# Moving the left operands of the weight products to other SBUF addresses in a two-layer graph kernel

## The chip, the cores and the metric

The kernel runs on one NeuronCore of one Trainium2 chip. The metric is the device time of one execution in microseconds. The kernel before takes 2596.89 us (median of three runs, 2596.37 to 2597.45). All timed runs told below were in the fast state; runs with a single time have no state of their own and are used for their traces only.

## The reference

For each of 128 graphs with 128 nodes and 512 features there are two layers. Cut to the products:

```
h  = relu(layernorm(x))
# layer 0: two hypergraph convolutions, H = (adj != 0)
xw = h @ W1.T                      # 512 -> 1024
h1 = relu(Dn * (H @ (Be * (H.T @ xw))) + b1);  h1 = layernorm(h1)
y  = Dn * (H @ (Be * (H.T @ (h1 @ W2.T)))) + b2   # 1024 -> 512
x  = x + (y + h)
# layer 1: mean aggregation
h  = relu(layernorm(x))
x  = x + relu(concat(h, (adj @ h) / deg) @ W.T)   # two 512 -> 512 products
```

## The kernel before

Each product with a weight is made of three passes in the type fp32r. In the trace of the kernel before, one fp32r matmul of 512 columns is one record and follows the last after 229 to 233 ns; py, a matmul of the same shape in full fp32, is two records of 428 ns each. An operand is split in a high part h, a low part l and a part d made of both, whose product brings in the cross terms, so each product is h with h, l with l, d with d. Per graph there are 24 such matmuls with w1 (left operand z), 24 with w2 (nh, nl, nd) and 24 with w3 (hh, hl, hd). Each multiplies a 128x128 left operand, which is loaded into the array (the records LDWEIGHTS, 128x128, in the trace), with 512 columns of weights, which stream through it (the records MATMUL, 128x512).

```
const = ctx.enter_context(tc.tile_pool(name="const", bufs=1))
pool = ctx.enter_context(tc.tile_pool(name="pool", bufs=1))
...
def parts(tag):
    return {m: const.tile([P, KH, 512], FP, name=tag + m) for m in "hld"}
w1, w2, w3 = parts("w1"), parts("w2"), parts("w3")
...
def product(left, w, k0, kk, main, name, between=None):
    wr = [w[m].bitcast(FR) for m in "hld"]
    pm, pd = bank(name + "m"), bank(name + "d")
    for i in range(2):
        for k in range(kk):
            nc.tensor.matmul(pm, left[i](k), wr[i][:, k0 + k, :], ...)
    main(pm)
    if between:
        between()
    for k in range(kk):
        nc.tensor.matmul(pd, left[2](k), wr[2][:, k0 + k, :], ...)
    return pd
```

In the names of the profile, rm and rd are the results with w1, gm and gd those with w2, bm, bd, am and ad those with w3. ps_s, pz, py and the second pair named ad (line 490) are full fp32 matmuls between them. A step of the loop works on several graphs at different stages and holds 86 matmul instructions.

## Time and profile before

| | kernel before |
|---|---|
| time | 2596.89 us |
| span of the profiled run | 2596.6 us |
| TensorE busy | 97% |
| VectorE, ScalarE, GpSimd busy | 80%, 72%, 53% |
| granted clock, mean | 0.989; 1.00 in the steady part |
| one step | 19.52 us |
| TensorE in the chain that ended last | 95% |

"Pitch" in what follows is the time from the start of one matmul to the start of the next. The lines, and how they are read, are in the prediction below.

### The profile page before, as it was taken

What the parts mean: (1) busy time and instruction counts of PE and PEld (TensorE: products, weight loads), DVE (VectorE), ACT (ScalarE), POOL (GpSimd) and SP (SyncE); (2) the same over time, 40 slices, a digit from 0 to 9 for tenths busy, and PEclk for the clock granted to TensorE, in tenths of its full rate; (3) what the DMA queues carried; (4) which work ended last, traced back from release to release, by engine and by line L of the source; (5) the groups of instructions that cost most, each with busy time, mean ns of one, the idle gap of its engine ahead of it and who ended that gap; (6) DMA issues with size and microseconds to landing.
All of it is one profiled execution on the core that took longest, in us unless ns stands there. A gap on an engine that the chain in (4) does not pass through costs nothing.

```text
span 2596.6 us, 38459 instructions
## 1 busy us (share of the span) xinstructions
PE 2529.4 (97%) x11024; PEld 1986.1 (76%) x11024; DVE 2076.6 (80%) x4519; ACT 1867.0 (72%) x3872; POOL 1368.7 (53%) x921
## 2 busy tenths in 40 slices
PE   4799999999999999999999999999999999999997
PEld 3577777777777777777777777777777777777775
DVE  7788888887888887887888888888887888888874
ACT  4677767777767777777777777777777777777773
POOL 5555455455455455455455455555555555555552
PEclk8899999999999999999999999999999999999998
DMA  4443443343443343443443343343343343344331
GB/s 117 115 124 115 127 124 115 127 125 115 126 124 116 125 126 112 126 128 113 126 125 115 125 126 117 121 125 121 118 129 119 118 128 121 115 128 123 115 123 64
DMA packets 410292, 311.71 MB, mean 120 GB/s; under 512 B 177376, under 2 KB 341216, under 8 KB 410080
## 3 DMA queue, kind: packets, MB, share of 16 engines
q1 hardware_dynamic: 409248, 309.19, 38.4%
q8 instruction: 87, 1.43, 0.2%
q14 instruction: 125, 1.02, 0.1%
q10 hardware_dynamic: 576, 0.07, 0.0%
q0 software_dynamic: 256, 0.01, 0.0%
HBM read 166.47 MB, written 142.61 MB: 119 GB/s over the span
## 4 chain that ended last, share of the span: by engine, by line
PE 95%; DVE 2%; DMA 1%; ACT 1%; SPq 1%; issue 0%; POOL 0%; DVEq 0%; POOLq 0%; ACTq 0%
PE gm L328 18%; PE rm L328 18%; PE bm L328 9%; PE am L328 9%; PE gd L334 9%; PE rd L334 9%; PE bd L334 5%; PE ad L334 5%; PE py L441 4%; PE pz L297 4%; PE ad L490 4%; PE ps_s L271 1%; DVE w2l L115 0%; DMA b_bc<-in_b_dram 0%; SPq L132 0%
## 5 line engine op out<-in xcount | busy, mean ns | idle before, releaser
L403 POOL TENSOR_TENSOR hl<-ht,hh 128x512 fp32r<-128x512 f32 x128 | 166.3, 1299 | 1058.8 <-DMA adjb<-in_adj_dram 659.7
L215 ACT ACTIVATE h<-x_t 128x512 f32<-128x512 f32 x256 | 162.0, 633 | 360.4 <-DVE x_t L444 310.4
L353 POOL TENSOR_TENSOR r<-r,b_bc 128x512 f32<-128x512 f32 x256 | 385.5, 1506 | 9.2 <-DVE r L352 7.0
L403 POOL TENSOR_TENSOR nl<-nt,nh 128x1024 fp32r<-128x1024 f32 x128 | 308.6, 2411 | 102.0 <-ACT nh L399 101.1
L347 ACT ACTIVATE r<-rm,dinv 128x512 f32<-128x512 f32 x256 | 175.1, 684 | 246.3 <-PE rm L328 246.2
L334 PE MATMUL gd<-w2d,nd 128*128 128x512 f32 x1024 | 310.4, 445 | 4.1 <-DVE nd L408 4.1
L328 PE MATMUL rm<-w1h,z 128*128 128x512 f32 x1024 | 290.5, 406 | 1.4 <-ACT z L304 1.4
L328 PE MATMUL rm<-w1l,z 128*128 128x512 f32 x1024 | 278.7, 394 | 1.7 <-ACT w1l L113 1.7
L334 PE MATMUL rd<-w1d,z 128*128 128x512 f32 x1024 | 277.5, 393 | 1.8 <-POOL w1d L118 1.8
L328 PE MATMUL gm<-w2h,nh 128*128 128x512 f32 x1024 | 262.0, 398 | 7.4 <-ACT nh L399 7.4
L334 PEld LDWEIGHTS gd<-w2d,nd 128*128 128x128 f32 x1024 | 193.1, 189 | 99.4 <-issue 30.9
L328 PE MATMUL gm<-w2l,nl 128*128 128x512 f32 x1024 | 260.0, 396 | 0.0
L328 PEld LDWEIGHTS gm<-w2h,nh 128*128 128x128 f32 x1024 | 193.7, 189 | 54.7 <-ACT nh L399 7.8
L310 DVE SCALAR_TENSOR_TENSOR z<-z 128x512 fp32r<-128x512 f32 x128 | 226.4, 1769 | 4.4
L328 PEld LDWEIGHTS gm<-w2l,nl 128*128 128x128 f32 x1024 | 192.5, 188 | 46.9 <-POOL nl L403 0.4
L334 PEld LDWEIGHTS rd<-w1d,z 128*128 128x128 f32 x1024 | 193.2, 189 | 45.4 <-POOL w1d L118 3.0
L328 PEld LDWEIGHTS rm<-w1l,z 128*128 128x128 f32 x1024 | 193.2, 189 | 45.3 <-ACT w1l L113 2.5
L226 ACT ACTIVATE h<-x_t,rs 128x512 f32<-128x512 f32 x256 | 208.3, 814 | 26.0 <-DVE rs L222 24.8
L328 PEld LDWEIGHTS rm<-w1h,z 128*128 128x128 f32 x1024 | 184.6, 190 | 34.8 <-ACT z L304 1.7
L352 DVE SCALAR_TENSOR_TENSOR r<-rd,dinv,r 128x512 f32<-128x512 f32 x256 | 190.4, 744 | 11.3 <-ACT r L347 2.2
L408 DVE SCALAR_TENSOR_TENSOR hd<-hh,hl 128x512 fp32r<-128x512 f32 x128 | 193.8, 1514 | 4.5 <-POOL hl L403 4.5
L307 DVE TENSOR_TENSOR z<-pz,z 128x512 fp32r<-128x512 f32 x128 | 88.5, 692 | 135.1 <-ACT z L304 135.1
(96 smaller groups left out, 5718.5 us busy)
## 6 DMA issues: line engine op xcount, KB each, us to landing
n_scratch<-r SPq DMA_DIRECT2D x128, 512.0 KB, 2.6
nb<-n_scratch SPq DMA_DIRECT2D x512, 128.0 KB, 2.8
x_t<-in_x_dram SPq DMA_DIRECT2D x128, 256.0 KB, 3.3
h_scratch<-h SPq DMA_DIRECT2D x128, 256.0 KB, 2.0
hb<-h_scratch SPq DMA_DIRECT2D x512, 64.0 KB, 2.0
out_dram<-x_t SPq DMA_DIRECT2D x128, 256.0 KB, 2.0
adj_t<-in_adj_dram SPq DMA_DIRECT2D x128, 64.0 KB, 1.9
an_scratch<-adj_t SPq DMA_DIRECT2D x128, 64.0 KB, 1.7
```

The lines of the kernel that those rows point to most:

```text
L215: copy(junk, src, func, accum_out=sm)
L226: copy(dst, src, func, bias=rs[:, 1:2], scale=rs[:, 0:1])
L297: nc.tensor.matmul(z[:, k * P : (k + 1) * P], H0[g][:, k * P : (k + 1) * P], S[g], start=True, stop=True)
L310: nc.vector.scalar_tensor_tensor(d, h, 2.0**-12, l, MUL, SUB)
L328: nc.tensor.matmul(pm, left[i](k), wr[i][:, k0 + k, :], start=(i == 0 and k == 0), stop=(i == 1 and k == kk - 1))
L334: nc.tensor.matmul(pd, left[2](k), wr[2][:, k0 + k, :], start=(k == 0), stop=(k == kk - 1), skip_group_check=True)
L347: lambda pm: copy(r, pm, AF.Copy, scale=dn[:, 1:2]), "r")
L352: nc.vector.scalar_tensor_tensor(r, PR.pop((g, half)), dn[:, 0:1], r, MUL, ADD)
L353: nc.gpsimd.tensor_tensor(r, r, b1_bc[:, cols], ADD)
L403: nc.gpsimd.tensor_tensor(SPLIT[key], a, h, SUB)
L408: nc.vector.scalar_tensor_tensor(t, h, 2.0**-12, low, MUL, SUB)
L441: nc.tensor.matmul(py, S.pop(g), G.pop(g), start=True, stop=True)
```

## The change

The change gives all left operands a pool of their own right behind the weights. The intent is that all start 32 bytes above a multiple of 64, as z alone did before. No instruction is added or removed.

```diff
     const = ctx.enter_context(tc.tile_pool(name="const", bufs=1))
+    left = ctx.enter_context(tc.tile_pool(name="left", bufs=1))
     pool = ctx.enter_context(tc.tile_pool(name="pool", bufs=1))
...
-            self.raw = pool.tile([P, n, 512], FP, tag=tag, name="raw")
+            self.raw = (pool if tag in "rA" else left).tile([P, n, 512], FP, tag=tag, name="raw")
...
-        Z[g] = z = pool.tile([P, 3, KD, P], FP, tag="z", name="z")
+        Z[g] = z = left.tile([P, 3, KD, P], FP, tag="z", name="z")
...
-        t = pool.tile([P, Q, width // P, B], FP, tag=tag, name=name + "b")
+        t = (left if tag == "t2" else pool).tile([P, Q, width // P, B], FP, tag=tag, name=name + "b")
...
-        nt = pool.tile([P, t.shape[2], P], FP, tag=tag, name=name + "t")
+        nt = left.tile([P, t.shape[2], P], FP, tag=tag, name=name + "t")
...
-            return pool.tile(shape, dtype, tag=tag, name=name).bitcast(FR)
+            return left.tile(shape, dtype, tag=tag, name=name).bitcast(FR)
...
-    eps_root = const.tile([P, 1], FP, name="eps_root")
+    eps_root = pool.tile([P, 1], FP, name="eps_root")
```

## The prediction

> **What bounds the kernel now.** I read the page first, then the table of stretches, then the chain of waits through one step, then TensorE's own timeline. The page and the table of stretches say whether anything but TensorE matters:
>
> ```profile
> PE 2529.4 (97%) x11024; PEld 1986.1 (76%) x11024; DVE 2076.6 (80%) x4519; ACT 1867.0 (72%) x3872; POOL 1368.7 (53%) x921
> ...
> PE 95%; DVE 2%; DMA 1%; ACT 1%; SPq 1%; issue 0%; POOL 0%; DVEq 0%; POOLq 0%; ACTq 0%
> ...
> 600.00:1100.00 500.00, 500.00 (x2206) 394.60 (x2205) 407.23 (x894) 369.10 (x769) 269.21 (x181) 1.00 0.39 121
> ```
>
> In the steady part TensorE is busy for all of the 500 us at a granted clock of 1.00, and the chain that ends last is TensorE for 95% of the span. VectorE, the next, is busy 407 of 500 us. So the time of the kernel is the sum of the pitches (start to start) of its matmuls, plus a head and a tail of some 135 us. The chain counts each piece without overlap, so one step (one of the 128 graphs in flight) can be read from it directly. Columns: start, us, engine and line, instructions.
>
> ```profile
> 1005.46 0.22 PE ps_s L271 x2
> 1005.68 1.85 PE rm L328 x8
> 1007.53 0.91 PE rd L334 x4
> 1008.44 1.83 PE rm L328 x8
> 1010.28 0.91 PE rd L334 x4
> 1011.19 0.86 PE py L441 x2
> 1012.05 0.89 PE pz L297 x8
> 1012.94 1.85 PE bm L328 x8
> 1014.79 0.93 PE bd L334 x4
> 1015.73 1.87 PE am L328 x8
> 1017.59 0.93 PE ad L334 x4
> 1018.53 3.73 PE gm L328 x16
> 1022.26 0.86 PE ad L490 x2
> 1023.12 1.86 PE gd L334 x8
> 1024.98 0.22 PE ps_s L271 x2
> ```
>
> From ps_s to the next ps_s is 1024.98 - 1005.46 = 19.52 us without a gap. The reader is to see one thing: the same instruction (128x128 left operand, 128x512 weights, one pass) does not have one price. The second rm with rd of the w1 product takes 1.83 + 0.91 = 2.74 us for 12, or 228.5 ns each. am with ad takes 1.87 + 0.93 = 2.80 us for 12, or 233.3 ns, and gm 3.73 us for 16, or 233.1 ns. The mean durations in the costliest groups (445 ns for gd, 406 for rm) do not show this: records of consecutive matmuls overlap, so a pitch has to be taken from starts.
>
> **Why the two prices differ.** In the built program all nine weight tiles start at 24,800 + n x 16,384 bytes in a partition, which is 32 above a multiple of 64. The left operand z starts at 216,992, also 32 above one. The other six start at multiples of 64: nd 189,696, nl 193,792, nh 197,888, hd 201,984, hh 204,032, hl 206,080. So in the kernel before, place and price go together: 32 above costs 229 ns, on the multiple 233.4. The single starts of the trace repeat it in the medians over 123 full steps: z's pitches cycle through about 229, 232 and 226 ns, the others' through 232 and 235. The head speaks for it too. There z runs with no other product before it, and at full clock it falls into its own cycle; w2 with nh does likewise into the other. It is confounded, though: z is also the only left operand of w1, and no trace of this kernel has w1 with another operand.
>
> At low clock both cost the same. Timeline of the head, while the clock is still down:
>
> ```profile
> 17.27 1.91 PE L328 MATMUL rm<-w1l,z 128*128 128x512 f32 x4
> ...
> 18.98 1.05 PE L334 MATMUL rd<-w1d,z 128*128 128x512 f32 x2
> ...
> 88.68 3.78 PE L328 MATMUL gm<-w2h,nh 128*128 128x512 f32 x8 [7.38 <-ACT nh L399]
> ...
> 92.26 2.23 PE L328 MATMUL gm<-w2l,nl 128*128 128x512 f32 x8
> ```
>
> z: (18.98 - 17.27) / 4 = 427 ns. nh: 92.26 - 88.68 = 3.58 us for eight, of which the first took 0.59 by its own starts, leaving 427 ns for each of seven. A penalty that shows only when columns stream at full rate looks like a collision of two reads of SBUF, the streaming weights and the left operand being loaded for the next matmul. That mechanism is my inference; the 4 ns are measured.
>
> **What the Trainium skill says.** "TensorE: Matmul & The Clock Gate", section "Back-to-back issue gap", gives N/2.4 + 2.5 ns for an isolated warm matmul, 216 ns at N = 512 (and about 131 per matmul in a sustained stream, which nothing here comes near). This trace shows 229 and 233, so 13 to 18 ns over the first figure, and at the low clock exactly its N/1.2 = 427. "SBUF — State Buffer", section "Who interferes with whom", gives TensorE two independent read ports, one for the moving operand and one for the load, and says that it never waits on anyone. The trace does not contradict that of other engines[...]. The same page, section "Operand start alignment", asks only for a multiple of the element size and says of its runs that they "timed nothing". So no page prices 32 against 64 bytes; the trace alone does.
>
> **The change, part by part.**
> 1. Instructions, order and waits: nothing changes. I compared the two built programs by engine, waits included, with line numbers and buffer numbers left out: no difference. Tags, and so the reuse of buffers, are the same; only pools, hence addresses, differ.
> 2. Addresses after: nd 172,256, nl 176,352, nh 180,448, hd 184,544, hh 186,592, hl 188,640, z 190,688. All seven are 32 above a multiple of 64. r, g, x_t and h0 move, but stay at multiples of 64; weights, s and ant keep their residue.
> 3. Matmuls that gain: 24 with w3 and 24 with w2 per graph, 48 x 128 = 6144 of the 11,024. If each paid z's steady price, the gain would be 233.4 - 229.1 = 4.3 ns x 6144 = 26 us.
> 4. What of it is lost at the start of a product: after a full fp32 matmul (pz, ps_s, L490) the pitch takes some matmuls to settle, and by the single starts z settles from above (233, 236, 229, 232) and hh from below (227, 235, 231, 229). So I compare like with like, by sums of the median starts. From the last fp32 pass, the 24 of w3 take 5.59 us, where z's 24 take 5.51: 0.08 saved. The 16 of gm take 3.736 us against 16 x 229.1 = 3.666: 0.07. The eight of gd take 1.861 us against z's first eight 1.852: 0.01. Sum 0.16 us per step of 19.52.
> 5. On the path: all of it, since TensorE has no idle in a step. 0.16 x 128 = 20.5 us, less a little for the head and the tail, where some 40 matmuls run at the low clock and gain nothing. 2597 - 20.5 = 2576.5; I take 2576.
> 6. Other work: the other engines get a step of 19.36 us and need at most 407/500 x 19.52 = 15.9 us of it (VectorE). Transfers that land in the moved raw tiles and nb now start 32 above a multiple of 64. hb already does, and lands in 2.0 us (64 KB) where nb takes 2.8 (128 KB), so I expect no cost; nb is not on the chain anyway.
>
> **Rivals.**
> A. The price belongs to w1, or to something else about z, not to the 32 bytes: the time stays at 2597. For it: the confounding named above. Against it: all nine weight tiles have the same residue and shape, and w2 and w3 agree with each other to 0.3 ns.
> B. What counts is the distance between left operand and weights, or a coarser multiple. Before, z was at 32 modulo 128 and the weights at 96; after, all are at 96, and their distance is a multiple of 2048 bytes. If the two reads then meet on the same place, pitches could rise for z as well: 72 x 4 ns x 128 = 37 us more, about 2634. Nothing in the trace shows such a case; small chance.
> C. The same, in the good direction: equal residues remove more of the 13 ns that z still pays over 216. If half of it went from all 72, 6.5 x 72 x 128 = 60 us would go beside the 20, to about 2517. Small chance too.
> D. Another engine becomes the bound, or the clock is throttled. VectorE has 18% of room and the clock is at 1.00 through the steady part, so no.
>
> **Range and chances.** About seven in ten for the mechanism, giving 2568 to 2582 according to how the products settle; two in ten for A near 2597; the rest for B and C. Eight times in ten the time should lie in 2566 to 2598. A change over 2% needs 52 us, which only C or a strong B could give: faster by over 2% 0.03, within 2% 0.94, slower by over 2% 0.03.
>
> **What would show it.** In the chain of the changed kernel, gm should take 3.66 to 3.68 us for 16 and am with ad 2.74 to 2.76 for 12, rm and rd unchanged, and a step 19.36 us; the durations on the other engines should stay. If gm stays at 3.73, rival A is right. If rm with rd moves from 2.74, the residue modulo 64 is not the whole rule.

## The result and the profile after

The changed kernel takes 2569.12 us (median of four runs, 2568.87 to 2570.42), the kernel before 2597.17 in the same rounds. The ratio is 0.9893, 95% interval 0.9876 to 0.9911. Ratios here are the mean time of one kernel's fast runs over that of the other's fast runs of the same rounds, so they are not quite the ratio of the medians quoted. A second measurement (run after_again) gave 2569.38 us and 0.9892. The gain is 28 us, 1.1%, inside the range and somewhat more than the 21 us forecast.

The chain of waits of the changed kernel, one step (start, us, engine and line, instructions; line numbers are one higher than before):

```profile
1013.95 0.22 PE ps_s L272 x2
1014.17 1.85 PE rm L329 x8
1016.02 0.91 PE rd L335 x4
1016.93 1.81 PE rm L329 x8
1018.74 0.91 PE rd L335 x4
...
1021.40 1.85 PE bm L329 x8
1023.24 0.92 PE bd L335 x4
1024.16 1.81 PE am L329 x8
1025.98 0.91 PE ad L335 x4
1026.88 3.62 PE gm L329 x16
...
1031.37 1.85 PE gd L335 x8
1033.21 0.22 PE ps_s L272 x2
```

The step is now 1033.21 - 1013.95 = 19.26 us. The reader is to see two things. First, am with ad takes 1.81 + 0.91 = 2.72 us for 12, 226.7 ns each, where 229 was expected. Second, the later rm with rd also takes 2.72 us, where it took 2.74. The w1 product has become cheaper too, although z was 32 above a multiple of 64 in both kernels. By single starts, the settled pitch is a constant 226.7 ns in all three products; the cycles of two and three values of the kernel before are gone.

The price of a product's start has not gone. After a full fp32 pass the pitches of the changed kernel run 229, 233, 236, 224, 231, 236, 228 and so on before they rest at 227. So the first eight of w1 and of w3 and all eight of gd still take 1.85 us.

The page's line on the chain and its row for the same 500 us as before:

```profile
PE 73%; ACT 9%; DVE 8%; DMA 4%; issue 3%; SPq 2%; POOL 1%; DVEq 0%; ACTq 0%; POOLq 0%
...
600.00:1100.00 500.00, 499.65 (x2231) 398.70 (x2230) 410.29 (x908) 372.80 (x778) 269.93 (x182) 1.00 0.41 124
```

TensorE was the chain for 95% of the span and is for 73% in this trace. That share is no property of the kernel: the same kernel, profiled again as after_again, has

```profile
PE 93%; DVE 2%; ACT 2%; DMA 1%; SPq 1%; issue 1%; POOL 0%; DVEq 0%; POOLq 0%; ACTq 0%
```

though it took 2568.57 us, as against 2569.05 us. A short wait can send the chain over the other engines for many steps back. What both traces show is that TensorE has begun to wait, though little: 499.65 of 500 us are busy here. One row of TensorE's waits, of the kernel before and then of the changed one (us in total, times, longest), and the chain at one such wait of the changed kernel:

```profile
PE py L441 <- POOL g L437: 7.7, 3, 3.6
```

```profile
PE py L442 <- POOL g L438: 10.5, 7, 3.9
```

```profile
933.49 3.33 DMA hb<-h_scratch
...
936.94 0.71 DVE ht L380
...
938.65 0.61 ACT hh L400
...
940.95 0.94 POOL g L438
...
941.94 1.12 PE py L442 x2
```

A transfer hb that usually lands in 2.0 us took 3.33; what depends on it came late and TensorE waited. Such slow landings are not new (the slowest hb took 3.9 us before and 4.0 after); what is new is that a step has less room for them. Added over the 122 steps between the first few and the end, the time above the median step is 0.20 us in the kernel before, 3.65 us in the changed one and 2.75 us in after_again. So the account for the two profiled executions is: 122 steps of 0.26 us less would be 31.7 us; 3.45 us of it were lost to new waits; head and tail became 1.4 us shorter. That makes 29.7 us, and the spans differ by 2596.6 - 2567.0 = 29.6 us. The timed medians differ by 28, because the profiled execution of the kernel before, 2598.55 us, was 1.4 us slower than the median.

### The profile page after: what moved, and what is told of

Its sections match the earlier page's. It is cut to its first block, busy times and chain, and to the rows that moved or that the text cites. A ratio compares the mean times of both kernels' runs of the same rounds, so it can differ in the third digit from the quotient of the medians.

```text
span 2567.0 us, 38459 instructions
## 1 busy us (share of the span) xinstructions
PE 2496.4 (97%) x11024; PEld 1982.6 (77%) x11024; DVE 2064.1 (80%) x4519; ACT 1866.1 (73%) x3872; POOL 1366.7 (53%) x921
## 4 chain that ended last, share of the span: by engine, by line
PE 73%; ACT 9%; DVE 8%; DMA 4%; issue 3%; SPq 2%; POOL 1%; DVEq 0%; ACTq 0%; POOLq 0%
PE gm L329 14%; PE rm L329 13%; PE bm L329 7%; PE am L329 7%; PE gd L335 7%; PE rd L335 7%; PE py L442 4%; PE bd L335 4%; PE ad L335 3%; PE pz L298 3%; PE ad L491 3%; DMA hb<-h_scratch 1%; DMA nb<-n_scratch 1%; ACT r L216 1%; ACT h L210 1%
## 5 line engine op out<-in xcount | busy, mean ns | idle before, releaser
L329 PE MATMUL gm<-w2h,nh 128*128 128x512 f32 x1024 | 255.6, 392 | 7.4 <-ACT nh L400 7.4
L329 PE MATMUL gm<-w2l,nl 128*128 128x512 f32 x1024 | 253.5, 390 | 0.0
```

The source lines that it names most:

```text
L329: nc.tensor.matmul(pm, left[i](k), wr[i][:, k0 + k, :], start=(i == 0 and k == 0), stop=(i == 1 and k == kk - 1))
```

## The experiments

Twelve kernels ran. The first four ask which property of the addresses counts. In e1 to e4, s1, s2 and f1 the built program has the same instructions, order and waits as the changed kernel (s1, s2 and f1 apart from how tiles are named and sliced). "Distance" below is the start of a left operand minus the start of its weights, modulo 256 unless another modulus is named. The pools were split into three (for nd to nh, for hd to hl, for z), with pads in front, and the weights could be moved by a pad before them:

```diff
-    left = ctx.enter_context(tc.tile_pool(name="left", bufs=1))
+    left = {c: ctx.enter_context(tc.tile_pool(name="left" + c, bufs=1)) for c in "thz"}
+    for c, pad in (("t", ...), ("h", ...), ("z", ...)):
+        if pad:
+            left[c].tile([P, pad // 4], FP, name="pad" + c)
...
+    pool.tile([P, 8], FP, name="padp")     # e1, e2, s1: keeps the tiles of pool on multiples of 64
...
+    const.tile([P, 8], FP, name="padw")     # only where the weights move by 32
```

**e1_swap: exchange the places of z and the others.** Pads of 192, 0 and 352 bytes: nd to hl at distance 192, z at 32.

> The left operands change places as seen from the weights: z (for w1) now starts 32 bytes past the residue of the weights modulo 512 and on a multiple of 64, as nd to hl did before; nd to hl start 192 past it, 32 above a multiple of 64, as z did before. Address theories (absolute residue or distance, both): the two prices change places, w1 products near 233.4 ns per matmul (12 in about 2.80 us), w2 and w3 products near 229.1 (16 of gm in 3.67 us), step about 19.42 us and time about 2584 us. Rival A of the prediction (w1 or z itself has the price): w1 stays at 229 or falls to 227 as in the changed kernel, w2 and w3 stay at 233.4, time near 2597 us.

Measured: 2586.83 us (one run), step 19.44 us. The chain:

```profile
1004.82 1.87 PE rm L333 x8
1006.69 0.93 PE rd L339 x4
...
1012.14 1.83 PE am L333 x8
1013.97 0.91 PE ad L339 x4
1014.88 3.66 PE gm L333 x16
```

The w1 product now pays 2.80 us for 12 (233.3 ns) and w3 2.74 (228.3); gm has come down to 3.66. The prices went with the addresses, so rival A of the prediction, that w1 or z itself had the price, is out.

**e2_all64: everything 32 bytes further.** Only the pad before the weights; the left pool follows. All operands are then on multiples of 64, and the distance stays 0.

> Weights and left operands all 32 bytes further than in the changed kernel: every one of them now starts on a multiple of 64 (left operands on a multiple of 128), and the distance of left operand to weights stays a multiple of 2048 bytes. Distance theory: 226.7 ns in every product, time as the changed kernel, 2569 us within 3. Absolute theory (left operands must lie 32 above a multiple of 64): 233.4 ns in all 72 products of a step, step near 19.62 us, time near 2610 us.

Measured: 2566.27 us (2565.39 to 2570.40), ratio 0.9882 (0.9868 to 0.9897). The chain has

```profile
1003.88 1.81 PE am L334 x8
1005.69 0.91 PE ad L340 x4
1006.60 3.63 PE gm L334 x16
```

which is 226.7 ns again for the 12 of w3. Lying 32 bytes above a multiple of 64 is not needed. The start of a product is another matter: after L496 (the changed kernel's L491) gd's pitches are 233 and 231 and then 227, where in the changed kernel all eight of gd stay unsettled, at the same distance of 0. So how long a product settles does not depend on the distance alone.

**e3_weights32: only the weights 32 bytes further.** The left operands keep their residue modulo 512, so the distance is 480 modulo 512, which is 224.

> Only the weights move by 32 bytes, to a multiple of 64; the left operands keep the residue of the changed kernel modulo 512 (32 above a multiple of 64, 96 modulo 128), so the distance becomes 480 modulo 512. Absolute theory: 226.7 ns as in the changed kernel, 2569 us. Distance theory: not 226.7; something like the 233.4 that the distance 32 had before, step 19.5 to 19.6 us, time 2595 to 2612 us.

Measured: 2609.90 us (2608.45 to 2611.08), ratio 1.0047 (1.0031 to 1.0064), step 19.62 us. The chain has

```profile
1012.47 1.87 PE rm L333 x8
1014.33 0.94 PE rd L339 x4
...
1022.62 3.74 PE gm L333 x16
```

2.81 us for 12 of w1 is 234 ns, 3.74 for 16 of w2 is 233.8 ns (233.3 by single starts, without the matmul at a product's end): all three products are slow now, although every left operand has the residue that the change aimed at. e2_all64 and e3_weights32 together decide for the distance and against the absolute place of the left operand.

**e4_far: three distances.** Pads of 64, 64 and 128 bytes: 64 for nd to nh, 128 for hd to hl, 256 for z.

> Weights as in the changed kernel; nd, nl, nh at a distance of 64 modulo 512 from them, hd, hh, hl at 128, z at 256. All stay 32 above a multiple of 64. If only the residue modulo 64 counts: all at 226.7 ns. If a modulus of 128 counts (z before had 64 modulo 128 and 229.1 ns): gm and gd at 229.1, w3 and w1 products at 226.7. If a modulus of 256: w1 alone at 226.7, w3 something else. If 512: none at 226.7. Time 2569 to 2600 us accordingly.

Measured: 2595.53 us (one run). w1 at 256 rests at 226.7 ns as at 0. w2 at 64 alternates between 231 and 236; w3 at 128 goes through a long cycle between 228 and 241, near 233 on average. All three are 32 above a multiple of 64, so the residue modulo 64 alone does not decide. Neither does a modulus of 128: 128 is not as good as 0. One of 256 fits.

**s1_fine and s2_fine: the remaining places.** The same pads with other values, and z sliced out of a slightly larger tile, so that it can start at any multiple of four bytes.

> Known so far, steady pitch by distance of left operand to weights modulo 256: 0 gives 226.7 ns, 32, 64 and 224 give 233.3 to 233.5, 128 about 233, 192 gives 229.2. Here nd to nh (w2) stand at 96, hd to hl (w3) at 160, z (w1) at 16. Theory: only the distance modulo 256 counts and 0 is the one good place: 96 and 160 lie between 229 and 234. At 16 the theory of whole 32-byte places says 226.7 (same place as 0), that of a finer grain says 229 to 234. If any of the three is under 226, a better place than that of the changed kernel exists.

> nd to nh (w2) stand at a distance of 128, hd to hl (w3) at 224, z (w1) at 240, modulo 256. Distance theory modulo 256, whatever the weight matrix: w2 at 128 as w3 had it (about 233 on average), w3 at 224 as all had it at 480 (233.3). A theory of modulo 512 would let w3 at 224 differ from 480. z at 240, 16 bytes short of the weights' place: 226.7 if 16 bytes do not matter on that side, 229 to 234 if they do.

Measured: 2594.46 and 2594.06 us (one run each, two of three products at bad places on purpose). In s1_fine, w2 at 96 took 233.8 ns, w3 at 160 233.4. z at 16 took 226.7 and, unlike at 0, from its second matmul on: its first twelve pitches are 313 and then 227 eleven times, where the changed kernel's are 318, 231, 236, 228, 233, 231 and only then 227. In s2_fine, w2 at 128 goes through the long cycle that w3 had there, w3 at 224 settles into the pitches of e3_weights32 to the ns (modulo 256, not 512), and z at 240 took 228.2. No place was under 226.7. The settled pitches, from the median starts over the 123 full steps of each trace (means over a cycle; where a cycle is cut moves them by up to 0.4 ns):

| distance modulo 256 | settled pitch, ns | product and run |
|---|---|---|
| 0 | 226.7 | all in the changed kernel and e2_all64; w1 in e4_far |
| 16 | 226.7, at once | w1 in s1_fine |
| 32 | 233.4 to 233.6 | w2, w3 before; w1 in e1_swap |
| 64 | 233.5 | w2 in e4_far |
| 96 | 233.8 | w2 in s1_fine |
| 128 | 232 to 233 | w3 in e4_far, w2 in s2_fine |
| 160 | 233.4 | w3 in s1_fine |
| 192 | 229.0 to 229.3 | w1 before; w2, w3 in e1_swap |
| 224 | 233.3 | all in e3_weights32; w3 in s2_fine |
| 240 | 228.2 | w1 in s2_fine |

Weights start on a multiple of 32 in all rows of the table.

**f1_all16: the distance 16 for all, by moving the weights.** It was meant as a kernel that beats both. A left operand is easily sliced at 16, but a shared tag is not, so I moved the weights: all nine in one tile that starts 16 bytes in.

```diff
+    pool.tile([P, 8], FP, name="padp")
+    flat = const.tile([P, 9 * KH * 512 + 8], FP, name="wall")[:, 4 : 4 + 9 * KH * 512]
+    every = flat.rearrange("p (w k c) -> p w k c", w=9, k=KH)
...
-        return {m: const.tile([P, KH, 512], FP, name=tag + m) for m in "hld"}
+        return {m: every[:, 3 * (int(tag[1]) - 1) + i] for i, m in enumerate("hld")}
```

> The changed kernel with every left operand 16 bytes past the place of the weights modulo 256 (all nine weight tiles in one tile that starts 16 bytes in; same instructions, order and waits). In the sweep z at 16 took 226.7 ns from its second matmul on, where at 0 it takes about ten to settle. If that holds for all: w1 saves 29 ns, w3 38 and gd 29 in a step, 96 ns together, step 19.16 us, time 2557 us. Rival: the step is by now so near to what the chain over DVE, ACT and the transfers needs that waits of py eat it: 2562 to 2569 us, not different from the changed kernel.

Measured: 2636.03 us (2635.09 to 2636.56), ratio 1.0149 (1.0132 to 1.0165), step 19.83 us. In the chain:

```profile
1013.31 3.79 PE gm L333 x16
```

That is 236.9 ns, by single starts an alternation of 234 and 239, 236.7 on average, in every product, with no wait added (instructions, order and waits are those of the changed kernel but for the names). Both theories of the expectation fell. At the same distance of 16, z in s1_fine took 226.7; the difference is that here the weights start 16 above a multiple of 32, and there z did. So the distance is not the whole rule: where the weights themselves start counts as well.

**after_again: the changed kernel in the same rounds.**

> The changed kernel itself, on the same chip and in the same rounds as f1_all16: 2569 us within 2, ratio to the kernel before 0.989.

Measured: 2569.38 us (2568.09 to 2571.01), ratio 0.9892 (0.9877 to 0.9906), as expected.

**f3_fine: 8 and 24 bytes.** f1_all16 with the tile cut at 24 bytes instead of 16, and z sliced 16 further.

> A finer grain: nd to hl at 8 bytes past the weights' place modulo 256, z at 24. If a grain of 32 bytes counts, all take 226.7 ns; if one of 16 bytes, w2 and w3 at 226.7 as at 0 with its settling, and z at 24 as at 16. Otherwise values between 226.7 and 233.4; a value under 226 would be a better place.

Measured: 2625.67 us (one run). w3 at 8 took 236.5 ns, w2 at 8 about 236, w1 at 24 233.3. Since the weights are off the multiple of 32 here too, the run does not answer what it was sent for. It agrees with f1_all16: in every product measured with weights off a multiple of 32 the pitch is between 233 and 237. Whether all weights off it are slow, with any left operand, is not shown.

**f4_next: which weights a left operand is measured against.** To tell a collision with the previous matmul's streaming from something about the pair itself, w1's high part and z's high part got steps of 2080 and 544 bytes from k to k in place of 2048 and 512.

```diff
+    odd = const.tile([P, 4 * 520 + 24 + 4 * 520], FP, name="w1h")   # two halves, step 520 elements
...
+        if w is w1:
+            left, wr = left[:1] * 3, [odd[k0 // KD].bitcast(FR)] * 3   # high parts thrice: wrong result
+            order, k0 = order[:: -1 if k0 else 1], 0
```

> Wrong results on purpose (w1 product with the high parts thrice), to tell which weights a left operand is measured against: its own, or those that stream while it is being loaded, which are the previous matmul's. In the first half of w1 each left operand stands at 0 from its own weights and at 32 (once in four at 160) from the previous ones; in the second half, with k reversed, at 32 from its own and at 0 (once in four at 128) from the previous ones. Theory that the load of the next left operand meets the streaming of the current weights: first half towards 233.4 ns, second half towards 226.7, with a longer pitch at most around every fourth. Theory of the own pair: the reverse, first half settling to 226.7, second half to 233.4. w2 and w3 are untouched controls at 226.7.

Measured: 2573.46 us (one run; the outputs still passed the comparison, presumably because the tripled product is normalised behind). In the chain the w1 product reads

```profile
1018.56 0.93 PE rd L345 x4
1019.49 1.84 PE rm L339 x8
1021.34 0.93 PE rd L345 x4
```

The second half, 2.77 us for 12, is 231 ns; the first half's settled matmuls, rd, take 231 too by single starts (0.93 us for four in the chain). w2 and w3 stay at 226.7. Neither half rests at 226.7 or at 233.4, so neither theory holds in its pure form. What it does show: an own distance of 0 in every matmul, as in the first half, does not suffice when the starts shift from one matmul to the next.

**e5_late_aggregate: one break fewer.** The full fp32 matmul of line 491 goes behind gd, so that gd follows gm directly.

```diff
-            conv2_weights(s - 1, between)
-        else:
-            between()
+            conv2_weights(s - 1, None)
+        between()
```

> The changed kernel with the full fp32 matmul of L491 (ad<-gb_t,ant) after the eight gd instead of between gm and gd, so that a step has two places instead of three where a product follows a full fp32 pass. Theory (the pitch has to settle after each such pass): gd takes 8 x 226.7 = 1.81 us instead of 1.85, w1 still settles; step 19.26 - 0.03 = 19.23 us, time 2565 us, 4 under the changed kernel. Rival (the settling belongs to the start of any product): no gain, 2569 us; or the later finish costs a wait and it gets slower than that.

Measured: 2725.78 us (2724.82 to 2726.66), ratio 1.0493 (1.0475 to 1.0510). From TensorE's waits:

```profile
PE py L442 <- POOL g L438: 122.2, 126, 5.5
```

The wait for g now comes in every step, 122 us in all, four times what the addresses gave. In the program VectorE's addition o (line 496), which needs the aggregate, stands ahead of its addition g (line 435), so a later aggregate makes g late. The trace shows, in one step, o waiting 1.13 us for the aggregate and starting at 1010.27 us, and g only at 1012.87. The median step is 1.26 us longer than in the changed kernel: by the single starts 1.05 us at the wait before py, 0.11 within py and 0.10 for the aggregate and gd. The expected gain is not there either: gd's first pitch is 332 ns, a gap of about 105, and the following ones are 231, 231, 233, 229, 231, 230 and 227. So the theory fell: gd pays a settling without a full fp32 pass before it; a short gap goes before it instead.

**e6_bias_first: take py's input out of the queue behind hl.**

```diff
-        do(layer1_low, s - 3)
         do(conv2_bias, s - 2)
+        do(layer1_low, s - 3)
```

> The changed kernel with the addition that py needs (conv2_bias, L438) before the subtraction hl (layer1_low, L404) on GpSimd. Theory: with the shorter step the changed kernel loses 3.65 us in some nine steps whose py waits for g, which stands behind hl, which waits for hh and so for the landing of hb; in front of hl it does not wait. Then those steps go, time 2565 to 2566 us. Rival: the lost time comes from a transfer that the whole step needs, the wait moves to bm on hl: 2569 us or a little over.

Measured: 2616.61 us (2612.45 to 2617.13), ratio 1.0070 (1.0055 to 1.0085), step 19.62 us. The waits of py did become fewer (5.0 us in two places), but hl, then hd, and all that stands behind hd on VectorE come later. TensorE is only 4% of the chain that ended last, VectorE 33% and ScalarE 30%. Between 1000 and 1060 us the chain is led by hd (9%) and goes by r, ScalarE's nh and GpSimd's nl to gm. In the median step the last nh has a pitch of 456 ns and the first nl one of 336, and the next five fall from 235 to 230 before 227 is reached. The order that the changed kernel inherited is the better one, and the 3.5 us of new waits were not won back.

No kernel was found that beats the changed one clearly. e2_all64 is 3 us under it by medians, but the intervals of the ratios (0.9868 to 0.9897 and 0.9877 to 0.9906) overlap. The distance 16 by moving the left operands only was measured for z alone.

## Why the prediction was right, and where it was off

- **The bound** was read correctly: TensorE without gaps, so a shorter pitch shows in full. e1_swap confirms it in the other direction, where exchanging the places exchanged the prices.
- **Instructions, order and waits** were the same, as built; the result is an effect of addresses alone.
- **The size (part 3 and 4 of the sum) was too small.** The step that failed is "If each paid z's steady price": the left operands did not take z's old price of 229.1 ns but 226.7. By sums of median starts the w3 product saved 0.101 us (0.08 predicted), gm 0.104 (0.07), gd 0.015 (0.01). To that comes 0.030 us of the w1 product, for which nothing was predicted. Together that is 0.25 of the 0.26 us that the step became shorter, against 0.16.
- **The rule behind it was wrong.** The prediction, like the change, took the residue modulo 64 for the cause, and set its own test: if rm with rd moves from 2.74 us, that residue is not the whole rule. It moved to 2.72. e2_all64, with all operands on multiples of 64, is as fast; e3_weights32, with the left operands 32 above one, is slower than the kernel before. The new pool brought the left operands to a distance of 0 modulo 256 from the weights, which is the good place; the 32 bytes came along. That the change helped was therefore luck: left operands 64 bytes further would have met the prediction's condition as well, and at that distance e4_far measured 233.5 ns for w2, no better than before.
- **Rival B's premise was right and its sign wrong; rival C had the sign.** B asked whether the distance counts and feared that equal places collide; equal places were, with those 16 apart in s1_fine, the best measured. C was nearest in kind, not in size: it expected equal residues to remove half of the 13 ns left above 216; they removed 2.4.
- **Rival D** was put aside with "no", by VectorE's busy time. For 28 us that was near enough, but the waits of 2.75 to 3.65 us are its beginning, and busy time does not show it: VectorE has 18% of room in both kernels, yet in e6_bias_first the exchange of two instructions on GpSimd made the median step 0.36 us longer.
- **Transfers:** nb's median landing went from 2.8 to 3.0 us, and in e2_all64, where nb is on a multiple of 64 again, it is 2.8. VectorE's wait for nb rose from 4.8 to 15.1 us over the run (12.1 in after_again, 9.6 in e2_all64). Whether this cost anything in the end is not shown, since the times of the two kernels cannot be told apart.

What stays open is the mechanism. That two reads of SBUF get into each other's way is argued, from the rest at 427 ns for either address at the low clock and from the dependence on a distance; f4_next was to show it and did not decide, and f1_all16 shows that a distance alone is not the rule.

## What to carry to other kernels

When TensorE is the bound, compare the pitches of equal matmuls by their starts; a difference with equal shapes is worth an experiment with addresses, which costs only a pad. Change one address at a time: the good place here was found by aiming at a residue that had nothing to do with it. And when the bound gets shorter by 1%, look whether the chain over the other engines is now close behind: here two small reorderings cost 156 and 47 us, against the gain of 28. Profile twice before reading much into the chain's shares: one kernel gave TensorE 73% and 93%.

## What the Trainium skill lacked or had wrong

- "SBUF — State Buffer", section "Operand start alignment": it gives legality alone. Here the start of a TensorE operand changed the pitch of the same instruction from 226.7 to 236.7 ns, and the whole kernel from 2569 to 2636 us with the same instructions, order and waits.
- "SBUF — State Buffer", section "Who interferes with whom": two independent read ports for TensorE, which never waits on anyone. Slowing by other engines was not looked for, but the addresses of the two operands of TensorE itself are not independent in price (why is open): 226.7 ns at a distance of 0 modulo 256, 229 at 192, 233 to 234 at 32, 64, 96, 160 and 224.
- "TensorE: Matmul & The Clock Gate", section "Back-to-back issue gap": 216 ns for an isolated warm matmul of 512 columns and about 131 in a sustained stream. In fp32r the settled pitch never fell under 226.7 ns here, and 131 was not approached. The section names no type; other types were not run here.
- No page that I read has the settling: after a full fp32 pass or a gap of about 0.1 us, three to ten matmuls, the first included, pass before the pitch rests at 226.7 (at distance 0; at 16 in s1_fine they rest from the second on). After the first they are between 224 and 236 ns, 231 on average in the changed kernel.
